# A selective-scan block on one core: decays of two states in one tile of two PSUM banks, and step sizes in the banks of the sums

## The chip, the core and the metric

The kernel runs on one core of a Trainium2 chip. The core has five engines that matter here, each with its own queue of instructions that it works off in order: PE multiplies matrices into PSUM, ACT applies functions to single elements, DVE does vector operations and scans, POOL does vector operations too, SP issues the DMAs. PSUM is used here as eight banks of 128 partitions x 512 float32 numbers. The metric is the device time in microseconds (us) of one execution: 11345.4 us is the median of three runs of the kernel before (11343.77 to 11359.79).

## What is computed

Eight images of 96 channels and 64 x 64 pixels go through a convolutional block with a selective scan, then through an attention block and a feed-forward block. The scan takes almost all the time. Each image is read as a sequence of L = 4096 pixels in four orders (k = 0 to 3: by windows row-wise, by windows column-wise, and both backwards). For each order, each of 192 channels d and each of 16 states n:

```python
dts, bs, cs = (x_dbl[:, :, :R], x_dbl[:, :, R:R + N], x_dbl[:, :, R + N:])
delta = jax.nn.softplus(dt_projs(dts) + dt_projs_b)
A = -jnp.exp(A_logs)
# one step in l
dA = jnp.exp(dt_i[..., None] * A)
hst = dA * hst + (dt_i * u_i)[..., None] * b_i[:, :, None, :]
y = jnp.einsum('bkdn,bkn->bkd', hst, c_i)
```

A decay dA and an input dt*u*b for every channel, state and pixel, a linear recurrence along the pixels, a product with c, and a sum over the states. What stands before the scan (norm, projections, a depthwise convolution) is called the front here, what follows it the back end.

## The kernel before, in words

**Units.** The work is cut into 256 units: 8 images x 2 pairs of orders x 2 directions x 8 chunks of T = 512 pixels. A unit holds 6 tiles (`TILES`, n = 0 to 5): for each half g of the states and each third j of the channels a tile `hb` of 128 partitions x 4 states x 512 pixels. The partitions are 64 channels x 2 states, so that four "states" m = 0 to 3 in the free dimension stand for eight of the reference's. A unit therefore has 24 slots, one per state of a tile, and 256 x 24 = 6144 scans are made in all.

**One slot** (lines 1112 to 1135). ACT computes the decay `exp(a * delta)` of the state two slots ahead into a bank of PSUM (`decays`, line 1055). DVE scans the present state (line 1123). Then the state has to be multiplied by c, and there are two ways:

- A *banked* state is scanned in place in its PSUM bank, and DVE multiplies it by c into `hb` (line 1125). ACT copies its last element into `carry` (line 1126), where the next unit's scan starts.
- A *plain* state is scanned into `hb`. When all four states of the tile are scanned, ACT copies the last elements (line 1131) and POOL multiplies the plain states of the tile by c in one instruction (`outputs`, line 948).

The table `BANKED` says how many states of each tile n are banked: 4, 0, 4, 0, 4 and 2, or 1 in the last tile in the first eight units of an image from the second image on. So it divides the products by c between DVE and POOL.

**The other steps of a unit.** `inputs` (line 942, POOL) multiplies b and dt*u for a whole tile, seven slots before its first scan. `sums` (line 962, PE) adds the states with a matrix of two identities in two accumulators, `y01` and `y2` (a bank each; tiles 0, 1, 3 and 4 in the first, 2 and 5 in the second); at the end it also adds the D*u term, or the y of the orders done before, from tiles that `before` (line 954) has loaded. `gather` (line 983, ACT) copies the two banks out, and a DMA stores them. `step_sizes` (line 901) makes softplus in six steps: a matmul into a bank `dt`, Abs, Exp and Ln on ACT, max-and-add on DVE (line 925), and the product with u on POOL (line 928). One call (a) makes 128 channels of a unit, another (b) the 64 remaining channels of two units. `spread` (line 930) copies the results into tiles that hold each channel twice, by DMA; `states` (line 873) loads b and c.

**Order.** The schedule is written out by hand: `plan` (line 997) puts each step of a unit u, of the unit before (`last`) and of the next two (`nxt`, `third`) into one of the 24 slots, and the engines' queues follow that order. Between the slots, `advance` (line 1086) issues the steps of two side streams: the back end of the image before and the front of the next image. Some of their activations need another function table; those are issued in the slots `CALM` = 0, 1, 8, 9, 16 and 17 alone (line 391). Requests for DMAs made by `later` go out three slots afterwards.

**Banks.** Of the eight banks, `da` has three (one state each, in rotation), `dt`, `f0`, `f1`, `y01` and `y2` one each; `f0` and `f1` serve the side streams.

Of the kernel before, what the change touches and what calls it, by code (L numbers as in the profile page):

```python
# [9 lines left out]
F32 = mybir.dt.float32  # L10
# [14 lines left out]
G = 4  # L25
# [8 lines left out]
BANKED = ((4, 0, 4, 0, 4, 1), (4, 0, 4, 0, 4, 2))  # L34
# [9 lines left out]
def kernel(ctx: ExitStack, tc: tile.TileContext, a, out):  # L44
# [16 lines left out]
    BANKS = {"da": 3, "dt": 1, "f0": 1, "f1": 1, "y01": 1, "y2": 1}  # L61
# [784 lines left out]
    for b in range(out.shape[0]):  # L846
        s = {"b": b, "done": set(), "live": b + 1 == out.shape[0]}
        images.append(s)
        for pair in (1, 0):
            for back in range(2):  # L850
                for i in range(NC):
# [4 lines left out]
                    u.bc, u.hb, u.delta, u.du = {}, {}, {}, {}  # L856
                    u.banked = BANKED[int(b == 0 or u.i % 32 >= NC)]
# [43 lines left out]
    def step_sizes(us, i):  # L901

        u, which = us[0], "ab"[len(us) - 1]
        if i == 0:
            u.ps = bank("dt", "dt")
# [42 lines left out]
    def outputs(u, n):  # L948

        lo = u.banked[n]  # L950
        hb = u.hb[n][:, lo:, :]
        nc.gpsimd.tensor_tensor(hb, hb, u.bc[1, TILES[n][0]][:, lo:, :], ALU.mult)  # L952

    def before(u):

        src = u.s["u"][1] if u.k == 1 else u.s["y"][u.pair]
        u.plain = []
        for i, rows in enumerate((slice(0, P), slice(P, src.shape[0]))):
            t = sp.tile([P, T], F32, tag=f"u{i}", name=f"u{i}", bufs=1)[: rows.stop - rows.start]
            u.plain.append(into(t, src[rows, bass.ts(u.c, T)]))  # L960

    def sums(u, ns, m):
# [12 lines left out]
        if ns[-1] == 5 and m == 1:  # L975
            first = u.k == 1
            for ps, w, x in (
                (u.p[0], dd_a if first else ident, u.plain[0]),
                (u.p[1][low] if first else u.p[1], dd_b if first else ident, u.plain[1]),
            ):  # L980
                nc.tensor.matmul(ps, w, x, start=False, stop=True, skip_group_check=True)  # L981
# [15 lines left out]
    def plan(u, last, nxt, third):  # L997
# [6 lines left out]
        if last:  # L1004
            put(0, outputs, last, 5)
            put(0, before, last)
            for m in range(2):
                put(m, sums, last, (3, 4), 2 + m)
            for m in range(2):
                put(5 + m, sums, last, (5,), m)  # L1010
            put(7, states, u, 1, 1)
            put(10, gather, last, 0)
            put(11, gather, last, 1)
# [4 lines left out]
        if third and u.i % 2:  # L1018
            put(16, step_sizes, (nxt, third), 5)
        put(8, outputs, u, 1)  # L1020
        put(16, outputs, u, 3)
        for m in range(4):
            put(13 + m, sums, u, (0, 1), m)
            if m < 2:
                put(18 + m, sums, u, (2,), m)
                put(22 + m, sums, u, (3, 4), m)
        if nxt:
            for i, slot in enumerate((0, 2, 4)):
                put(slot, step_sizes, (nxt,), i + 3)
            put(4, spread, nxt, 0, (0, 1))  # L1030
# [194 lines left out]
```

## Time and profile before

| | |
|---|---|
| median of three runs | 11345.4 us |
| the profiled execution | 11372.4 us, of which the profile's span is 11370.7 us |
| first to last scan | 351.6 to 11090.8 us |
| DVE busy, POOL busy, ACT busy | 10367.4 us, 10398.7 us, 7508.4 us |
| products by c on POOL (L952) | 512 of 4 states, 4529 ns each; 56 of 3, 3452 ns; 200 of 2, 2365 ns |
| products by c on DVE (L1125) | 3528 of one state, 692 ns each |
| scans (L1123) | 6144 |
| copies of ends on ACT | 3528 of one column (157 ns), 768 of a tile |
| mean granted clock of PE | 0.82 of full speed |

A line of the page's groups reads so: the source line, the engine, the operation, output tile <- input tiles, partitions x elements and type of both, the number of instructions; then their busy time in us and the mean length of one in ns; then the idle time of the engine just before them and what ended most of it. A line of the waits reads: who waited, <- for whom, then total us, number of waits, and the longest in us. A line of the timeline reads: start in us from the span's start, length in us, engine, line, operation, tiles; in brackets the idle time before it and what ended it. The page counts idle time on an engine only where nothing ran on it; two instructions of one engine can overlap, so the distance between starts can be shorter than a length.

### The profile page before, as it was taken

Reading aid. Unit: us, or ns where it says so; the run is one execution under the profiler, and the core shown is the slowest. Engines: PE = TensorE matmul, PEld = TensorE weight load, DVE = VectorE, ACT = ScalarE, POOL = GpSimd, SP = SyncE. Lnnn points to the kernel's source line nnn. Section 1 sums busy time; section 2 is a strip of 40 time slices with the busy share of each in tenths; the row PEclk is TensorE's granted clock in tenths of the full one; section 3 lists DMA queues with packets and bytes.
Section 4 is the critical chain, followed back from the end, with each engine's and each line's share of the span. In section 5 each row is a group of like instructions: output and inputs, shape, how many; then the busy total and the mean of one; then the engine's idle time right before and its main releaser. Section 6 shows DMA issues by size and latency. Waiting matters only on the chain. (4 is left out here: it accounts for less than half of the span.)

```text
span 11370.7 us, 97041 instructions
## 1 busy us (share of the span) xinstructions
PE 8567.3 (75%) x23270; PEld 2328.5 (20%) x23270; DVE 10367.4 (91%) x10828; ACT 7508.4 (66%) x14939; POOL 10398.7 (91%) x2783
## 2 busy tenths in 40 slices
PE   6577657887778877888678876788768887676677
PEld 2111112222122211222112221222212221111122
DVE  0799999999999999999999999999999999999991
ACT  3566656767666676667766676666766667666674
POOL 0799999999999999999999999999999999999990
PEclk8678778888788877889778887888878888787787
DMA  2788878898888888888888888889888888888872
GB/s 71 171 197 197 201 189 210 209 225 196 203 210 212 219 198 202 210 215 215 195 207 210 216 214 194 210 205 228 202 200 211 212 220 195 198 198 195 201 188 78
DMA packets 1081039, 2253.24 MB, mean 198 GB/s; under 512 B 419609, under 2 KB 420314, under 8 KB 949395
## 3 DMA queue, kind: packets, MB, share of 16 engines
q1 hardware_dynamic: 1080467, 2247.05, 81.3%
q8 instruction: 184, 3.01, 0.1%
q14 instruction: 388, 3.18, 0.1%
HBM read 1507.14 MB, written 336.69 MB: 162 GB/s over the span
## 5 line engine op out<-in xcount | busy, mean ns | idle before, releaser
L946 POOL TENSOR_TENSOR hb<-b,du 128x2048 f32<-128x2048 f32 x1536 | 6939.0, 4535 | 21.3 <-DMA du<-ua 14.3
L1062 ACT ACTIVATE da<-delta,w_a_logs 128x512 f32<-128x512 f32 x6144 | 4216.7, 689 | 696.3 <-DVE hb L1123 575.8
L972 PE MATMUL p<-hb,halves 128*64 128x512 f32 x12288 | 3822.7, 731 | 800.1 <-POOL hb L952 382.1
L1123 DVE TENSOR_TENSOR_SCAN da<-da,carry,hb 128x512 f32<-128x512 f32 x3087 | 3949.0, 1279 | 58.0 <-ACT da L1062 54.3
L952 POOL TENSOR_TENSOR hb<-hb,c 128x2048 f32<-128x2048 f32 (+2 forms) x768 | 2984.9, 3887 | 304.7 <-ACT carry L1131 252.2
L1123 DVE TENSOR_TENSOR_SCAN hb<-da,carry,hb 128x512 f32<-128x512 f32 x2289 | 2781.0, 1264 | 57.7 <-ACT da L1062 56.7
L1125 DVE TENSOR_TENSOR hb<-da,c 128x512 f32<-128x512 f32 x3528 | 2440.5, 692 | 154.0 <-DVE da L1123 0.9
L1126 ACT COPY carry<-da 128x1 f32<-128x1 f32 x3528 | 554.9, 157 | 2351.6 <-DVE hb L1125 2341.1
L972 PEld LDWEIGHTS p<-hb,halves 128*64 128x64 f32 x12288 | 916.2, 161 | 3540.7 <-issue 2129.5
L434 PE MATMUL conv<-f0im,taps 97*128 97x512 f32 (+1 forms) x2088 | 903.5, 664 | 95.9 <-ACT f0pre L490 54.3
L928 POOL TENSOR_TENSOR ua<-nat,ua 128x512 f32<-128x512 f32 x256 | 327.3, 1279 | 257.5 <-DMA b<-xd 257.5
L1123 DVE TENSOR_TENSOR_SCAN da<-da,hb 128x512 f32<-128x512 f32 x441 | 537.7, 1219 | 26.0 <-POOL hb L946 24.6
L925 DVE SCALAR_TENSOR_TENSOR nat<-dt,nat 128x512 f32<-128x512 f32 x384 | 259.5, 676 | 238.9 <-ACT nat L923 238.9
L911 PE MATMUL dt<-dts,dt_w 7*64 7x512 f32 (+1 forms) x1024 | 450.0, 657 | 16.9 <-DVE nat L925 12.4
L981 PE MATMUL p<-u,ident 128*128 128x512 f32 x768 | 438.3, 699 | 3.6 <-DMA u<-y 3.6
L376 PE MATMUL ctr<-f1b,cen_c 96*96 96x512 f32 x460 | 271.9, 697 | 193.4 <-DVE f1b L769 158.8
L434 PEld LDWEIGHTS conv<-f0im,taps 97*128 97x128 f32 (+1 forms) x2088 | 254.6, 174 | 681.6 <-issue 523.5
L1123 DVE TENSOR_TENSOR_SCAN hb<-da,hb 128x512 f32<-128x512 f32 x327 | 377.9, 1204 | 4.9 <-ACT da L1062 4.9
L382 PE MATMUL var<-f1b,ones_c 96*96 96x512 f32 x346 | 207.4, 684 | 153.6 <-ACT f1b L379 145.3
L792 POOL TENSOR_TENSOR f1b<-f1b,f1o 96x512 f32<-96x512 f32 x58 | 67.7, 1167 | 252.0 <-ACT f1o L790 251.9
L1131 ACT COPY carry<-hb 128x4 f32<-128x4 f32 (+2 forms) x768 | 146.8, 191 | 197.4 <-DVE hb L1123 184.8
L655 PE MATMUL cab<-f1m,cab_w 96*96 96x512 f32 x348 | 206.0, 719 | 90.9 <-ACT f1b L664 41.4
(416 smaller groups left out, 7710.5 us busy)
## 6 DMA issues: line engine op xcount, KB each, us to landing
b<-xd SPq DMA_DIRECT2D x1024, 512.0 KB
c<-xd SPq DMA_DIRECT2D x1024, 512.0 KB
delta<-nat SPq DMA_DIRECT2D x1536, 128.0 KB
du<-ua SPq DMA_DIRECT2D x1024, 128.0 KB
y<-yt SPq DMA_DIRECT2D x512, 256.0 KB
u<-y SPq DMA_DIRECT2D x384, 256.0 KB
ua<-u SPq DMA_DIRECT2D x256, 256.0 KB
du<-ub SPq DMA_DIRECT2D x512, 128.0 KB
```

The source lines that it names most:

```text
L376: nc.tensor.matmul(ps, cen_c, src, start=i == 0, stop=i == len(srcs) - 1)
L434: nc.tensor.matmul(ps, taps[:, t, lo : lo + n], im[:, r0 + dy : r0 + dy + 8, dx : dx + HW], start=t == 0, stop=t == 8,)
L911: nc.tensor.matmul(ps, dt_w[32 * w.k : 32 * w.k + R + 1, d], w.dts, start=True, stop=True)
L928: nc.gpsimd.tensor_tensor(x, u.nat, x, ALU.mult)
L946: nc.gpsimd.tensor_tensor(hb, u.bc[0, g], u.du[j].unsqueeze(1).to_broadcast([P, G, T]), ALU.mult)
L952: nc.gpsimd.tensor_tensor(hb, hb, u.bc[1, TILES[n][0]][:, lo:, :], ALU.mult)
L972: nc.tensor.matmul(ps, halves, u.hb[n][:, i, :], start=TILES[n][0] == 0 and m == 0, stop=False, skip_group_check=True)
L981: nc.tensor.matmul(ps, w, x, start=False, stop=True, skip_group_check=True)
L1062: nc.scalar.activation(da[q], u.delta[j], AF.Exp, scale=a_neg[:, u.k, j, g * G + m : g * G + m + 1])
L1123: nc.vector.tensor_tensor_scan(dd if banked else x, dd, x, 0.0 if u.start else col, ALU.mult, ALU.add)
L1125: nc.vector.tensor_tensor(hb[:, m, :], d, u.bc[1, g][:, m, :], ALU.mult)
L1126: kept.append(lambda col=col, d=d, at=first_at: nc.scalar.copy(col, d[:, at : at + 1]))
```

## The change

Four things change together. The decays of two states go into one tile of two neighbouring banks, of which two rotate (four banks instead of three); each scan still takes one state, but the product with c of two banked states is one instruction of 1024 elements, and one copy on ACT takes both ends. The bank `dt` goes: call (a) of the step sizes uses `y01`, call (b) `y2`, between the eviction of one unit's sums and the start of the next one's. For that, `plan` is laid out anew: the evictions come at slots 4 and 8, the step sizes between 6 and 20, the loads and DMAs move with them, and the sum of tiles 0 and 1 starts a slot later. And the table gives more states to DVE: the last tile has 2 banked states, and 4 in every second unit in the larger part of the images. In each `put` the first argument is the slot.

```diff
@@ -31,7 +31,7 @@
 SPREAD = 5
 HB = 6
 
-BANKED = ((4, 0, 4, 0, 4, 1), (4, 0, 4, 0, 4, 2))
+BANKED = (((4, 0, 4, 0, 4, 2),), ((4, 0, 4, 0, 4, 2), (4, 0, 4, 0, 4, 4)))
 
 HOLD = 3
 LAND = 11
@@ -58,7 +58,7 @@
     dram = ctx.enter_context(tc.tile_pool(name="scratch", bufs=2, space=DRAM))
     psum = ctx.enter_context(tc.tile_pool(name="psum", bufs=1, space=PSUM))
 
-    BANKS = {"da": 3, "dt": 1, "f0": 1, "f1": 1, "y01": 1, "y2": 1}
+    BANKS = {"f0": 1, "f1": 1, "y01": 1, "y2": 1}
 
     def bank(tag, name):
         return psum.tile([P, T], F32, tag=tag, name=name, bufs=BANKS[tag])
@@ -853,8 +853,9 @@
                     u.s, u.pair, u.back, u.k = s, pair, back, pair + 2 * back
                     u.c, u.start = (NC - 1 - i if back else i), i == 0
                     u.new, u.i = (pair, back, i) == (1, 0, 0), len(units)
-                    u.bc, u.hb, u.delta, u.du = {}, {}, {}, {}
-                    u.banked = BANKED[int(b == 0 or u.i % 32 >= NC)]
+                    u.bc, u.hb, u.delta, u.du, u.plain = {}, {}, {}, {}, {}
+                    some = BANKED[int(b == 0 or u.i % 32 >= NC)]
+                    u.banked = some[u.i % len(some)]
                     units.append(u)
 
     TILES = [(g, j) for g in range(2) for j in range(3)]
@@ -902,7 +903,7 @@
 
         u, which = us[0], "ab"[len(us) - 1]
         if i == 0:
-            u.ps = bank("dt", "dt")
+            u.ps = bank({"a": "y01", "b": "y2"}[which], "dt")
             if which == "a":
                 todo = [(u.ps, slice(0, P), u)]
             else:
@@ -948,16 +949,24 @@
     def outputs(u, n):
 
         lo = u.banked[n]
+        if lo == G:
+            return
         hb = u.hb[n][:, lo:, :]
         nc.gpsimd.tensor_tensor(hb, hb, u.bc[1, TILES[n][0]][:, lo:, :], ALU.mult)
 
-    def before(u):
+    def before(u, i):
 
         src = u.s["u"][1] if u.k == 1 else u.s["y"][u.pair]
-        u.plain = []
-        for i, rows in enumerate((slice(0, P), slice(P, src.shape[0]))):
-            t = sp.tile([P, T], F32, tag=f"u{i}", name=f"u{i}", bufs=1)[: rows.stop - rows.start]
-            u.plain.append(into(t, src[rows, bass.ts(u.c, T)]))
+        rows = (slice(0, P), slice(P, src.shape[0]))[i]
+        t = sp.tile([P, T], F32, tag=f"u{i}", name=f"u{i}", bufs=1)[: rows.stop - rows.start]
+        u.plain[i] = into(t, src[rows, bass.ts(u.c, T)])
+
+    def added(u, i):
+        ps, first = u.p[i], u.k == 1
+        w = ((dd_a, dd_b)[i]) if first else ident
+        nc.tensor.matmul(
+            ps[0:64] if first and i else ps, w, u.plain[i], start=False, stop=True, skip_group_check=True
+        )
 
     def sums(u, ns, m):
 
@@ -972,13 +981,6 @@
             nc.tensor.matmul(
                 ps, halves, u.hb[n][:, i, :], start=TILES[n][0] == 0 and m == 0, stop=False, skip_group_check=True
             )
-        if ns[-1] == 5 and m == 1:
-            first = u.k == 1
-            for ps, w, x in (
-                (u.p[0], dd_a if first else ident, u.plain[0]),
-                (u.p[1][low] if first else u.p[1], dd_b if first else ident, u.plain[1]),
-            ):
-                nc.tensor.matmul(ps, w, x, start=False, stop=True, skip_group_check=True)
 
     def gather(u, i):
 
@@ -1003,54 +1005,61 @@
 
         if last:
             put(0, outputs, last, 5)
-            put(0, before, last)
             for m in range(2):
                 put(m, sums, last, (3, 4), 2 + m)
+            put(2, added, last, 0)
+            put(4, gather, last, 0)
             for m in range(2):
                 put(5 + m, sums, last, (5,), m)
+            put(6, added, last, 1)
+            put(8, gather, last, 1)
             put(7, states, u, 1, 1)
-            put(10, gather, last, 0)
-            put(11, gather, last, 1)
+        if nxt:
+            put(2, spread, nxt, 0, (0, 1))
+            put(3, spread, nxt, 1, (0, 1))
+        if third:
+
+            put(5, fetched_u, third)
+            for i, slot in enumerate((6, 8, 9, 10, 12, 20)):
+                put(slot, step_sizes, (third,), i)
+            if u.i % 2:
+                for i, slot in enumerate((9, 11, 12, 13, 15, 16)):
+                    put(slot, step_sizes, (nxt, third), i)
         for n in range(6):
             to = (u, n + 2) if n < 4 else (nxt, n - 4)
             if to[0]:
                 put(4 * n + 1, inputs, *to)
-        if third and u.i % 2:
-            put(16, step_sizes, (nxt, third), 5)
         put(8, outputs, u, 1)
         put(16, outputs, u, 3)
-        for m in range(4):
-            put(13 + m, sums, u, (0, 1), m)
+        for m, slot in enumerate((14, 15, 16, 16)):
+            put(slot, sums, u, (0, 1), m)
             if m < 2:
                 put(18 + m, sums, u, (2,), m)
                 put(22 + m, sums, u, (3, 4), m)
+        put(18, before, u, 0)
+        put(21, before, u, 1)
         if nxt:
-            for i, slot in enumerate((0, 2, 4)):
-                put(slot, step_sizes, (nxt,), i + 3)
-            put(4, spread, nxt, 0, (0, 1))
-            put(6, spread, nxt, 1, (0, 1))
             put(10, states, nxt, 0, 0)
             put(15, states, nxt, 1, 0)
             put(20, states, nxt, 0, 1)
             if u.i % 2 == 0:
                 put(15, spread, nxt, 0, (2,))
                 put(16, spread, nxt, 1, (2,))
-        if third:
-            put(1, fetched_dt, third)
-            put(9, fetched_u, third)
-            for i, slot in enumerate((20, 22, 23)):
-                put(slot, step_sizes, (third,), i)
-            if u.i % 2:
-                for i, slot in enumerate((9, 11, 12, 13, 15)):
-                    put(slot, step_sizes, (nxt, third), i)
+            else:
                 put(17, spread, nxt, 0, (2,))
                 put(18, spread, nxt, 1, (2,))
-            elif u.i + 3 < len(units):
-                put(21, fetched_pair, third, units[u.i + 3])
+        fourth = at_index(u.i + 3)
+        if fourth:
+            put(14, fetched_dt, fourth)
+            if u.i % 2 == 0:
+                put(21, fetched_pair, third, fourth)
         return at
 
     def at_index(i):
         return units[i] if 0 <= i < len(units) else None
+
+    def column(j, g, m):
+        return 8 * j + g * G + m
 
     def decays(q):
 
@@ -1058,12 +1067,13 @@
             return
         u, (n, m) = units[q // 24], divmod(q % 24, G)
         g, j = TILES[n]
-        da[q] = bank("da", "da")
+        if m % 2 == 0:
+            da[q // 2] = psum.tile([P, 2, T], F32, tag="da", name="da", bufs=2)
         nc.scalar.activation(
-            da[q], u.delta[j], AF.Exp, scale=a_neg[:, u.k, j, g * G + m : g * G + m + 1]
+            da[q // 2][:, m % 2, :], u.delta[j], AF.Exp, scale=a_neg[:, u.k, j, g * G + m : g * G + m + 1]
         )
 
-    da, kept, side, carry = {}, [], [], None
+    da, kept, side, carry = {}, [], [], [None]
     for u in units[:2]:
         fetched_dt(u)
     fetched_u(units[0])
@@ -1076,12 +1086,43 @@
     for what in range(2):
         spread(units[0], what, range(3))
     fetched_u(units[1])
-    for i in range(3):
-        step_sizes(units[1:2], i)
     inputs(units[0], 0)
     inputs(units[0], 1)
     decays(0)
     decays(1)
+    for i in range(6):
+        step_sizes(units[1:2], i)
+    fetched_dt(units[2])
+
+    def scanned_state(u, slot):
+
+        n, m = divmod(slot, G)
+        g, j = TILES[n]
+        q, hb = 24 * u.i + slot, u.hb[n]
+        end = slice(0, 1) if u.back else slice(T - 1, T)
+        while kept:
+            kept.pop(0)()
+        decays(q + 2)
+        pair = da[q // 2]
+        d, x = pair[:, m % 2, :], hb[:, m, :]
+        banked = m < u.banked[n]
+        if u.back:
+            d, x = d[:, ::-1], x[:, ::-1]
+        col = column(j, g, m)
+        init = 0.0 if u.start else carry[0][:, col : col + 1]
+        nc.vector.tensor_tensor_scan(d if banked else x, d, x, init, ALU.mult, ALU.add)
+        if m % 2 == 0:
+            return
+        del da[q // 2]
+        if banked:
+            nc.vector.tensor_tensor(hb[:, m - 1 : m + 1, :], pair, u.bc[1, g][:, m - 1 : m + 1, :], ALU.mult)
+            ends, lo, hi = pair, m - 1, m + 1
+        elif m == G - 1:
+            ends, lo, hi = hb[:, u.banked[n] :, :], u.banked[n], G
+        else:
+            return
+        to = carry[0][:, column(j, g, lo) : column(j, g, hi)].unsqueeze(2)
+        kept.append(lambda: nc.scalar.copy(to, ends[:, :, end]))
 
     def advance(n):
 
@@ -1103,33 +1144,14 @@
                 final = back_end(b, u.s)
                 last_kit = back_kit(None, "f0", True, kit_f)
                 side.append(Stream(final[0][0](last_kit, range(1, NC)[::-1])))
-        if third and third.new:
+        if u.i + 3 < len(units) and units[u.i + 3].new:
             drained(*side[-1:])
             all_issued()
         if u.start:
-            carry = sp.tile([P, 24], F32, tag="carry", name="carry")
+            carry[0] = sp.tile([P, 24], F32, tag="carry", name="carry")
         todo = plan(u, last, nxt, third)
         for slot in range(24):
-            n, m = divmod(slot, G)
-            g, j = TILES[n]
-            q, hb, first_at = 24 * u.i + slot, u.hb[n], 0 if u.back else T - 1
-            col = carry[:, 8 * j + g * G + m : 8 * j + g * G + m + 1]
-            while kept:
-                kept.pop(0)()
-            decays(q + 2)
-            d = da.pop(q)
-            banked = m < u.banked[n]
-            dd, x = (d[:, ::-1], hb[:, m, ::-1]) if u.back else (d, hb[:, m, :])
-            nc.vector.tensor_tensor_scan(dd if banked else x, dd, x, 0.0 if u.start else col, ALU.mult, ALU.add)
-            if banked:
-                nc.vector.tensor_tensor(hb[:, m, :], d, u.bc[1, g][:, m, :], ALU.mult)
-                kept.append(lambda col=col, d=d, at=first_at: nc.scalar.copy(col, d[:, at : at + 1]))
-            elif m == G - 1:
-                lo = 8 * j + g * G
-                kept.append(
-                    lambda c=carry[:, lo + u.banked[n] : lo + G].unsqueeze(2), h=hb[:, u.banked[n] :, :], at=first_at:
-                    nc.scalar.copy(c, h[:, :, at : at + 1])
-                )
+            scanned_state(u, slot)
             for f, args in todo[slot]:
                 f(*args)
             place[0] = slot
...
```

More of the change, by code (lines that the diff above doesn't have):

```diff
@@ L1140 @@
     outputs(u, 5)
-    before(u)
     for m in range(2):
@@ L1145 @@
         sums(u, (5,), m)
+    for i in range(2):
+        added(u, i)
     gather(u, 0)
```

## The prediction

> **What bounds the kernel now.** I read the page from the top: the engines' shares, the slices, the groups by line; then the waits of DVE and of POOL, and a stretch of the timeline. The chain that ended last has 2% of the span and carries nothing here.
>
> ```profile
> PE 8567.3 (75%) x23270; PEld 2328.5 (20%) x23270; DVE 10367.4 (91%) x10828; ACT 7508.4 (66%) x14939; POOL 10398.7 (91%) x2783
> ```
> Two engines are full; the slices show 9 for both except at the ends. Their groups, and ACT's largest:
>
> ```profile
> L946 POOL TENSOR_TENSOR hb<-b,du 128x2048 f32<-128x2048 f32 x1536 | 6939.0, 4535 | 21.3 <-DMA du<-ua 14.3
> L1062 ACT ACTIVATE da<-delta,w_a_logs 128x512 f32<-128x512 f32 x6144 | 4216.7, 689 | 696.3 <-DVE hb L1123 575.8
> ...
> L1123 DVE TENSOR_TENSOR_SCAN da<-da,carry,hb 128x512 f32<-128x512 f32 x3087 | 3949.0, 1279 | 58.0 <-ACT da L1062 54.3
> ...
> L1125 DVE TENSOR_TENSOR hb<-da,c 128x512 f32<-128x512 f32 x3528 | 2440.5, 692 | 154.0 <-DVE da L1123 0.9
> ```
> Which of the two leads is in DVE's waits:
>
> ```profile
> DVE hb L1123 <- ACT da L1062: 61.6, 90, 1.4
> ...
> DVE da L1123 <- ACT da L1062: 54.3, 22, 6.0
> ...
> DVE da L1123 <- POOL hb L946: 25.1, 8, 20.2
> ```
> DVE hardly waits for POOL; POOL waits 252.2 us for L1131, the copy of ends that follows DVE's scans. So **DVE leads** and POOL is close behind. From the first scan to the last (351.6 to 11090.8 us) DVE's gaps sum to 338 us: 117 end with a decay, 25 with POOL, most of the others with an input from ACT or PE for the neighbouring images' work.
>
> What a state costs DVE is read from starts, since its instructions overlap:
>
> ```profile
> 5016.39 1.28 DVE L1123 TENSOR_TENSOR_SCAN da<-da,carry,hb 128x512 f32<-128x512 f32 x1
> 5016.51 0.16 ACT L1126 COPY carry<-da 128x1 f32<-128x1 f32 x1 [1.63 <-DVE hb L1125]
> 5016.70 0.69 ACT L1062 ACTIVATE da<-delta,w_a_logs 128x512 f32<-128x512 f32 x1
> ...
> 5017.71 0.69 DVE L1125 TENSOR_TENSOR hb<-da,c 128x512 f32<-128x512 f32 x1
> ...
> 5018.31 1.28 DVE L1123 TENSOR_TENSOR_SCAN da<-da,carry,hb 128x512 f32<-128x512 f32 x1
> ```
> The product needs the scan's result and starts 1.32 us after it (median over the trace 1.316). The next scan needs nothing of the product and starts 0.60 later (median 0.608), before the product has ended. Scans into hb, which don't depend on each other, follow at 1.176. A banked state thus takes 1.924 us of DVE, a plain one 1.176. ACT's copy and decay come after the product has ended: that releases the bank.
>
> **DVE's work.** The new table makes 156 units of 14 banked states and 100 of 16: 3784 instead of 3528. At the old price 256 more cost 256 x 0.748 = +191 us. Pairing changes the price. In the order of the changed kernel's instructions the second scan of a banked pair waits for the first one's end, because both write one tile. The trace has no scan waiting for a scan; its ends are 1.176 (free) and 1.316 (as the product waits). A wait for a result of the same length is the nearer row: 1.316. The product of 1024 elements has rows on both sides, 692 ns at 512 and 1957 ns at 1728 (L227), so 1.22 us long; from start to next start 0.608 + 0.533 (512 elements at the 1.04 ns of these rows) = 1.141, or 1.22 if nothing overlaps. I take 1.141. A pair: 1.316 + 1.316 + 1.141 = 3.773, against 2 x 1.924 = 3.848: 0.075 less, times 1892 pairs = -142. In 165 pairs another instruction stands between the scans and hides the 0.14 of the wait: -23. **Sum +26 us.** Ends: 1727 x 0.14 = 242 less with a free wait, 1892 x 0.08 = 150 more without overlap.
>
> [...] But the row of starts shows that the fixed part is half covered already (0.608 between starts, not 0.692), so 0.075 is left, and I use the row.
>
> **POOL's work.** 200 products of two states and 56 of three become 156 of two; from the rows by shape (4529, 3452, 2365 ns) 2985 - 2688 = 297 us less. DVE gains only its 25 us of gaps behind POOL: **-25**.
>
> **The decays' lead.** This is where I expect the loss. Before, three banks rotate and a scan waits for its own decay; ACT may be two states ahead. After, two pairs rotate. A pair's first decay waits until the pair before last is multiplied and its ends are copied, and the first scan of a pair waits for both decays (the order's waits show it). Between the two decays stands everything ACT has to do in the even slot. From the start of a pair's first scan, ACT can begin after 0.11, copies (0.19), makes two decays (0.69 + 0.72, the second waits for the first): 1.71 us. A banked pair lasts 3.77 and leaves 2.06 for other work, a plain one 2.35 and leaves 0.64 (0.83 without copy). The largest other work is a table load, an activation, a table load: 1.29 + 1.50 + 1.29 = 4.08 us, in quiet slots. Before, it had 3 x 1.924 less 1.84 (start and copies 0.49, two decays 1.35) = 3.93 us and cost 0.15; now, in an even slot, it costs 2.0. Taking the ACT rows that stand between the two decays in the order, with their intervals from the trace, they exceed what is left in 61 of 1891 banked windows, by 116 us together (53 of them such bursts), and in 148 of 1180 plain ones, by 65. That is 181 us. Of the 117 of today 35 end at slot 11, where ACT itself waits for PE, and stay; 82 are replaced. **+99.** Ends: +30, if the bursts meet idle stretches; +190, since work after the second decay, left out here, can push the next pair too. ACT gains 1636 copies less (0.19 each, 311 us); these are taken into the windows.
>
> **Banks of the sums.** The step sizes' product moves from slot 20 to slot 6 of the same unit, into y01, and b's takes y2. So the sums must be evicted at slots 4 and 8 instead of 10 and 11. Behind the copy at slot 8 stand on ACT the Abs of the step sizes, which waits for its PE product, and the next decays. Today ACT waits 6.6 us in all for L981: there was room. Read in the timeline for the fourth image, the last tile-5 sum ends after the next unit's slot 8 begins in 9 units of 32, on average 1.5 us after. Then come one added product and the dt product (1.1 each), against 1.1 us that the pair has left beside copy and Abs: up to 1.7 us each, 9 x 8 x 1.7 = 122; nothing, if PE, with one added product less ahead, is on time. PE loses work there, so I take under half: **+55**. Sums (0,1) start a slot later and end close to where POOL refills their buffer (slot 17); POOL's 297 us hide it, and without them two or three units in 32 would cost about 1 us each.
>
> **Moved at no cost.** The other steps of a (Abs to max-add) come at 8 to 12 instead of 22 to 2; ACT's are counted in the windows, DVE's is the same instruction. POOL's ua product moves from slot 4 to slot 20 before, seven slots (12 us) ahead of the DMA that takes it. Delta and du go out at slots 2 and 3, not 4 and 6: SP's 1951.7 us of waiting for L925 go, which nothing that DVE waits for was behind. The u and y loads (18, 21) have 8 slots, some 14 us, until their product; dts (14) has 16, ua (5) 15. Were such a load late, SP's queue behind it would be, and the sums. The front stages end in unit 26 of an image, before the drain, which now comes at 29 instead of 30.
>
> Sum: 26 + 99 + 55 - 25 = +155 us. The profiled execution took 11372.4, with 11370.7 of span, 27 above the median 11345.4; I add the step to the median: **11500**.
>
> **Rivals.**
> *POOL sets the pace through others.* DVE's gaps other than for decays are 221 us; if POOL's fullness stands behind them (POOL was busy 284.32 of 284.32 us in the window from 6822 us; PE waits 382.1 for L952), they go: 11345 + 26 - 221 = 11150. Against it: the gaps end with ACT and PE results of side work. It decides if decays cost under 195.
> *The second scan's wait is nearly free.* 11500 - 242 = 11258. [...] Against: the product[...] waits 1.316.
> *It cancels.* The copies saved give ACT room for its bursts: 11345 + 26 - 25 = 11346. Against: the buffers, not ACT's load, bound the lead.
> *The tight order costs more.* Upper ends, 26 + 190 + 122 - 25: 11660, and to 11800 with the product unoverlapped.
>
> **Chances.** Main case 11400 to 11600: 0.60; tight order 0.22; cancels 0.07; POOL 0.05; free wait 0.06. What this kernel's measurement can tell is about 0.2%: same is 11323 to 11368. Faster 0.11, same 0.06, slower 0.83. The range for 8 in 10, 11340 to 11680, leaves out the two faster cases and the tail of the tight one.
>
> **What would show it.** In the new profile: starts of two banked scans 1.32 apart and 1.14 from product to next scan; DVE's busy time about as now; POOL's near 10100; DVE waiting 200 us or more for decays, at even slots only, above all 2, 10 and 18; ACT waiting for the added product. Wrong if DVE's wait for decays stays near 116, or DVE's scans of a pair start 1.18 apart.

## The result, and the profile after

The changed kernel takes **11480.7 us** (median of four runs, 11471.39 to 11484.81), the kernel before 11350.56 beside it (four runs, 11343.77 to 11359.79). The ratio is 1.0115, with a 95% interval of 1.0102 to 1.0127: 130 us slower, where 155 were forecast.

The profiled execution has a span of 11469.7 us, 99 more than the one before. From the first scan to the last it takes 10861.6 us (351.8 to 11213.3) instead of 10739.2: **+122**. Behind the last scan it takes 256.4 instead of 279.9. That part is 256 to 266 in the later runs too, and 256 in one that keeps the old layout (`e6_order_alone`), so most of the 27 us by which the profiled execution of before lay above its median seems to stand there. The 122 us between the scans are what has to be explained.

The page's first part, and its costliest groups:

```profile
PE 8559.5 (75%) x23270; PEld 2303.9 (20%) x23270; DVE 10415.6 (91%) x9192; ACT 7268.9 (63%) x13203; POOL 10109.5 (88%) x2683
...
L947 POOL TENSOR_TENSOR hb<-b,du 128x2048 f32<-128x2048 f32 x1536 | 6926.7, 4527 | 46.9 <-PE p L981 22.8
L1113 DVE TENSOR_TENSOR_SCAN da<-da,carry,hb 128x512 f32<-128x512 f32 x3336 | 4285.1, 1285 | 247.1 <-ACT da L1072 150.5
L1072 ACT ACTIVATE da<-delta,w_a_logs 128x512 f32<-128x512 f32 x6144 | 4227.9, 689 | 396.8 <-DVE hb L1113 263.1
...
L1118 DVE TENSOR_TENSOR hb<-da,c 128x1024 f32<-128x1024 f32 x1892 | 2317.1, 1225 | 95.9 <-DVE da L1113 0.9
```

DVE executes 1636 instructions fewer and is busy 48 us longer. POOL has lost 289 us, and ACT 240. The idle time before the banked scans has grown from 58.0 us to 247.1, and the decays end most of it. In the waits of DVE, where both kinds of scan and the largest wait for side work between the scans stand:

```profile
DVE da L1113 <- ACT da L1072: 150.5, 99, 4.7
...
DVE f1b L571 <- ACT f1b L570: 52.7, 80, 2.6
DVE hb L1113 <- ACT da L1072: 46.6, 55, 2.9
```

From the start of the first scan to that of the last, decays end 201 us of DVE's gaps instead of 117, and POOL 12 instead of 5. All gaps in this stretch sum to 390 us instead of 318, **+72**; the rest of the 122 us, **+51**, is DVE's own work (gaps under 0.04 us, such as the one before a product, count as work). A wait for POOL before the first scan, 20.2 us in the kernel before and 2.4 now, stands outside this stretch. POOL now waits behind DVE (before, 252.2 us):

```profile
POOL hb L955 <- ACT carry L1125: 595.8, 278, 7.8
```

How a pair goes, in the timeline of DVE (rows alike that follow each other are joined, so x2 with 2.62 us is two scans):

```profile
4997.10 2.62 DVE L1113 TENSOR_TENSOR_SCAN da<-da,carry,hb 128x512 f32<-128x512 f32 x2 [1.12 <-ACT da L1072]
4999.75 1.22 DVE L1118 TENSOR_TENSOR hb<-da,c 128x1024 f32<-128x1024 f32 x1
5000.89 2.61 DVE L1113 TENSOR_TENSOR_SCAN da<-da,carry,hb 128x512 f32<-128x512 f32 x2
5003.53 1.22 DVE L1118 TENSOR_TENSOR hb<-da,c 128x1024 f32<-128x1024 f32 x1
```

The product starts 2.65 us after the first scan, and the next scan 1.14 after the product's start. Two scans of a pair start 1.316 us apart (median of 1727), two scans into `hb` 1.190: the second of a pair does wait for the first. And the 1.12 us of idle time in the first row is what the prediction feared. ACT's timeline just before shows its cause:

```profile
4991.80 0.69 ACT L1072 ACTIVATE da<-delta,w_a_logs 128x512 f32<-128x512 f32 x1
4992.50 1.28 ACT L397 ACT_TABLE_LOAD   x1
4993.80 0.68 ACT L631 ACTIVATE gm<-cab,cab_b 64x512 f32<-64x512 f32 x1
4994.50 1.28 ACT L397 ACT_TABLE_LOAD   x1
4995.79 0.69 ACT L490 ACTIVATE f0pre<-conv,cb_a 128x512 f32<-128x512 f32 x1
4996.38 0.68 ACT L1072 ACTIVATE da<-delta,w_a_logs 128x512 f32<-128x512 f32 x1
```

The first and the last row are the decays of one pair. Between them stand two table loads and two activations of the side streams, 3.9 us. The scan at 4997.10 needs only the first of the two decays for its arithmetic, yet it starts when the second is ready (4996.38 + 0.68 = 4997.06), since both lie in one tile.

### The profile page after: what moved, and what is told of

Its sections match the earlier page's. It is cut to its first block, busy times and chain, and to the rows that moved or that the text cites. A ratio compares the mean times of both kernels' runs of the same rounds, so it can differ in the third digit from the quotient of the medians.

```text
span 11469.7 us, 93727 instructions
## 1 busy us (share of the span) xinstructions
PE 8559.5 (75%) x23270; PEld 2303.9 (20%) x23270; DVE 10415.6 (91%) x9192; ACT 7268.9 (63%) x13203; POOL 10109.5 (88%) x2683
## 5 line engine op out<-in xcount | busy, mean ns | idle before, releaser
L1113 DVE TENSOR_TENSOR_SCAN da<-da,carry,hb 128x512 f32<-128x512 f32 x3336 | 4285.1, 1285 | 247.1 <-ACT da L1072 150.5
L981 PE MATMUL p<-hb,halves 128*64 128x512 f32 x12288 | 3627.0, 710 | 684.3 <-DVE nat L926 467.3
L955 POOL TENSOR_TENSOR hb<-hb,c 128x2048 f32<-128x2048 f32 (+1 forms) x668 | 2685.9, 4021 | 601.5 <-ACT carry L1125 595.8
L1113 DVE TENSOR_TENSOR_SCAN hb<-da,carry,hb 128x512 f32<-128x512 f32 x2040 | 2496.9, 1265 | 49.8 <-ACT da L1072 44.8
L1118 DVE TENSOR_TENSOR hb<-da,c 128x1024 f32<-128x1024 f32 x1892 | 2317.1, 1225 | 95.9 <-DVE da L1113 0.9
L1125 ACT COPY carry<-da 128x2 f32<-128x2 f32 x1892 | 300.6, 159 | 2704.4 <-DVE hb L1118 2703.0
L912 PE MATMUL dt<-dts,dt_w 7*128 7x512 f32 (+1 forms) x1024 | 520.2, 769 | 385.3 <-ACT yt L994 210.8
L1125 ACT COPY carry<-hb 128x4 f32<-128x4 f32 (+1 forms) x668 | 129.5, 194 | 455.7 <-DVE hb L1113 438.6
L618 PE MATMUL cab<-f1im,cab_w 97*32 97x512 f32 x1044 | 283.0, 665 | 24.7 <-DVE f1pad L597 17.3
L929 POOL TENSOR_TENSOR ub<-nat,ub 128x512 f32<-128x512 f32 x128 | 162.7, 1271 | 140.1 <-DVE nat L926 137.3
```

The costliest lines, as they stand in the source:

```text
L618: nc.tensor.matmul(ps[at : at + 32, :], cab1_w[:, t, :], k.im.t[:, 8 * q + dy : 8 * q + dy + 8, dx : dx + HW], start=t == 0, stop=t == 8, ...
L912: nc.tensor.matmul(ps, dt_w[32 * w.k : 32 * w.k + R + 1, d], w.dts, start=True, stop=True)
L929: nc.gpsimd.tensor_tensor(x, u.nat, x, ALU.mult)
L981: nc.tensor.matmul(ps, halves, u.hb[n][:, i, :], start=TILES[n][0] == 0 and m == 0, stop=False, skip_group_check=True)
L1113: nc.vector.tensor_tensor_scan(d if banked else x, d, x, init, ALU.mult, ALU.add)
L1118: nc.vector.tensor_tensor(hb[:, m - 1 : m + 1, :], pair, u.bc[1, g][:, m - 1 : m + 1, :], ALU.mult)
```

## The experiments

My theory before these runs was the prediction's: the joined tile costs through the decays' lead, since one tile for two states makes a scan wait for both decays and binds the second scan to the first, and the table costs because DVE, not POOL, is the bound. The rival: the new layout with its early evictions costs, and the pairing is worth having. All times are medians of four runs (ten for `e4_table_14`), each with the median of the kernel before on the same chip.

### Single banks instead of pairs

Same layout and table; the four banks are four tiles, and every state has its own product and copy again.

```diff
-    BANKS = {"f0": 1, "f1": 1, "y01": 1, "y2": 1}
+    BANKS = {"da": 4, "f0": 1, "f1": 1, "y01": 1, "y2": 1}
...
-        if m % 2 == 0:
-            da[q // 2] = psum.tile([P, 2, T], F32, tag="da", name="da", bufs=2)
+        da[q] = bank("da", "da")
...
-            nc.vector.tensor_tensor(hb[:, m - 1 : m + 1, :], pair, u.bc[1, g][:, m - 1 : m + 1, :], ALU.mult)
+            nc.vector.tensor_tensor(hb[:, m, :], d, u.bc[1, g][:, m, :], ALU.mult)
```

> The changed layout and table, but each decay has a bank of its own (four in rotation) and each banked state its own product straight after its scan, as before. Pairing's part alone is undone. Theory (DVE's work and ACT's lead set the time): a banked state costs 1.924 us of DVE again, 165 us more than the pairs in all; the waits for decays fall from 201 us to about 50, since a scan waits for its own decay alone and four banks rotate. Together about +15: 11495 us (11440 to 11560). Rival (the loss lies in the new layout of evictions and step sizes): the waits stay near 200 us and DVE's extra work comes on top: 11645.

Measured: 11422.1 us, before 11352.0, ratio 1.0063 (1.0048 to 1.0078). That is below the expected range: DVE works 119 us more than in the changed kernel, not 165, and the gaps fell by more than was expected of the decays alone. Decays end 54 us of the gaps:

```profile
DVE da L1111 <- ACT da L1071: 30.6, 18, 3.3
...
DVE hb L1111 <- ACT da L1071: 22.8, 22, 3.3
```

All gaps are 213 us instead of 390. So **joined tile and joined product together lose 176 us of waiting for 119 us of work saved**. That the sum over both is still above before must come from the table or the layout.

### The table, and the layout

Here the second entry of the table is taken back, so that all units have 14 banked states:

```diff
-BANKED = (((4, 0, 4, 0, 4, 2),), ((4, 0, 4, 0, 4, 2), (4, 0, 4, 0, 4, 4)))
+BANKED = (((4, 0, 4, 0, 4, 2),), ((4, 0, 4, 0, 4, 2),))
```

> The changed kernel with 14 banked states in every unit. Theory (DVE is the bound): 100 units have two banked states less, each pair 3.773 - 2.352 = 1.42 us, so DVE has 142 us less and the time falls by about as much, 11340 us (11310 to 11400), although POOL gets 100 products of 2365 ns more (10346 us busy). Rival (POOL is the bound): no gain, or up to 200 us slower.

Measured: 11328.9 us, before 11352.0, ratio 0.9979 (0.9970 to 0.9988), 152 us less than the changed kernel. 100 pairs of states went back to POOL, and DVE's work between the scans fell by 142 us, the 1.42 us a pair that was expected. POOL's busy time rose by 227 us and cost nothing; it ends 9 us of DVE's gaps, where it ended 12: **DVE is the bound, POOL had room**.

```profile
PE 8576.4 (76%) x23270; PEld 2301.0 (20%) x23270; DVE 10279.1 (91%) x9092; ACT 7260.2 (64%) x13203; POOL 10336.8 (91%) x2783
```

The next has single banks as the first experiment, and the table of before: the layout, with one bank more for decays, is all that is left of the change.

```diff
-BANKED = (((4, 0, 4, 0, 4, 2),), ((4, 0, 4, 0, 4, 2), (4, 0, 4, 0, 4, 4)))
+BANKED = (((4, 0, 4, 0, 4, 1),), ((4, 0, 4, 0, 4, 2),))
```

> e1_single_banks with the table of before (14 banked states, 13 in 56 units): of the change only the new layout is left, which frees a bank, so that four single decays rotate. Theory: 256 states fewer on DVE at 0.748 us are 191 us less than e1, and the waits for decays stay near 54 us, against 117 before: about 11240 us (11200 to 11290), a gain over the kernel before of some 110; then the loss of the change is table and pairing together. Rival (the early evictions cost as much as the fourth bank gains): 11330 or more.

Measured: 11220.2 us, before 11343.6, ratio 0.9888 (0.9874 to 0.9903). Decays' waits are 52 us, all gaps 200 instead of 318. The layout is not what costs; with a fourth single bank it gains. The layout with three banks was not run, so the two parts of this gain are not told apart; the waits for decays are 65 of the 118 us of gaps that went.

So the change comes apart into three, each taken against the kernel before on its own chip:

| step | us |
|---|---|
| layout, and a fourth bank for single decays (`e5_layout_alone`) | -123 |
| 256 more states multiplied by DVE (to `e1_single_banks`: +70) | +193 |
| decays and products of two states joined (to the changed kernel: +130) | +60 |

### What the joined product itself is worth

The tiles stay joined; only the product is split again. This is the direct test of the price that the prediction took from the row of starts, 0.075 us a pair. If joining saved the whole fixed part of a product, it would be 0.159: an estimate from two lengths of the trace before, 692 ns at 512 elements and 1957 at 1728, which is 1.04 ns an element and 0.159 us beside them.

```diff
-            nc.vector.tensor_tensor(hb[:, m - 1 : m + 1, :], pair, u.bc[1, g][:, m - 1 : m + 1, :], ALU.mult)
+            for i in range(2):
+                nc.vector.tensor_tensor(hb[:, m - 1 + i, :], pair[:, i, :], u.bc[1, g][:, m - 1 + i, :], ALU.mult)
```

> The changed kernel, its pair of decays in one tile as it is, but the product of a pair in two instructions of 512. Nothing else moves. Theory (of the fixed part of a product only what isn't overlapped is saved): 0.590 + 0.608 us between starts in e2 against 1.141, 0.06 to 0.075 us per pair, 1892 pairs: 110 to 140 us slower than the changed kernel, 11605 us (11570 to 11640). [...]

Measured: 11586.5 us, before 11354.5, ratio 1.0204 (1.0189 to 1.0219): 106 us more than the changed kernel, 0.056 us for each of 1892 products. In the profiles DVE's work between the scans grows by 117 us, 0.062 each, and the gaps are 346 us instead of 390. In DVE's timeline of this kernel:

```profile
5004.65 2.61 DVE L1113 TENSOR_TENSOR_SCAN da<-da,carry,hb 128x512 f32<-128x512 f32 x2
5007.30 1.29 DVE L1119 TENSOR_TENSOR hb<-da,c 128x512 f32<-128x512 f32 x2
```

Two products take 1.29 us from start to end, not twice 0.69; the pair starts 2.65 us after its scans as before, and the next scan starts 1.20 after the first product, where the joined one leaves 1.14. So joining does not save the whole fixed part of 0.159 us: the second of two products starts 0.60 us after the first, 0.09 before that one has ended.

This run also splits the last row of the table. Against `e1_single_banks` it has the same products of one state, and DVE's work is the same (10589 and 10591 us), but the tiles and the copies of the ends are joined: 164 us slower, and in the profiles the gaps are 346 us instead of 213. So the joined tile costs about 160 us and the joined product gains about 100, each taken against the kernel before on its own chip.

### The other way to use four banks: scan, scan, product, product

If the wait of an instruction for the one just before it costs 0.14 us (1.316 against 1.176), it is better to separate them than to join them. With single banks, the two scans don't depend on each other, and neither do the products; each product then stands one instruction behind its scan. The four single tiles are made as in the first experiment.

```diff
...
         if m % 2 == 0:
             return
-        del da[q // 2]
+        ds = [da.pop(q - 1), da.pop(q)]
         if banked:
-            nc.vector.tensor_tensor(hb[:, m - 1 : m + 1, :], pair, u.bc[1, g][:, m - 1 : m + 1, :], ALU.mult)
+            for i, d in enumerate(ds):
+                nc.vector.tensor_tensor(hb[:, m - 1 + i, :], d, u.bc[1, g][:, m - 1 + i, :], ALU.mult)
...
```

> As e1_single_banks, but the order on DVE is scan, scan, product, product, each state with its own tile. No instruction then follows directly the one it waits for. Theory (0.14 us is lost wherever a dependent instruction follows its source at once, and the joined product saves only 0.075): two states take 2 x 1.176 + 2 x 0.608 = 3.568 us, 388 us less than the pairs, 530 less than e1. DVE's work falls under POOL's 10110 us, so that POOL joins in as bound: about 11050 us (10950 to 11150), with scans of a pair starting 1.18 apart. Rival (one product of 1024 elements is what pays): slower than the changed kernel, 11600.

Measured: **10932.6 us**, before 11352.0, ratio 0.9632 (0.9616 to 0.9648), better than expected. Its first line on the page and its DVE timeline:

```profile
PE 8368.8 (77%) x23270; PEld 2267.0 (21%) x23270; DVE 10121.0 (93%) x11084; ACT 7215.2 (66%) x15095; POOL 10103.4 (93%) x2683
```

```profile
5001.58 2.46 DVE L1111 TENSOR_TENSOR_SCAN da<-da,carry,hb 128x512 f32<-128x512 f32 x2
5003.94 1.27 DVE L1117 TENSOR_TENSOR hb<-da,c 128x512 f32<-128x512 f32 x2
5005.13 2.46 DVE L1111 TENSOR_TENSOR_SCAN da<-da,carry,hb 128x512 f32<-128x512 f32 x2
```

From pair to pair it takes 3.55 us instead of 3.78: scan to scan 1.190, scan to product 1.175, product to product 0.590, product to scan 0.594 (medians). DVE has 1892 instructions more than in the changed kernel and is busy 295 us less. Against the single states of the first experiment (1.317 + 0.608 each) a state costs 0.15 us less; times 3784 that is 568, and 490 came out: DVE's work between the scans fell by 522 us, and the gaps grew from 213 to 238.

The run of the last section, `e9_product_split`, gives DVE the same scans and products in the same order. Only the tiles of two states and the joined copies of their ends are different there, and it takes 654 us more: in the profiles 520 of work and 109 of gaps. With joined tiles the second scan starts 1.316 us after the first and the product 1.325 after the second scan, and the order gains nothing; with single tiles the same two intervals are 1.190 and 1.175. So in this order **the joined tile is what costs**, for it makes each of these instructions wait for the one just before it.

The same order alone, in the kernel before: three single banks, the old layout, table and bank `dt`. The decay of the state after next must here wait for the products, so its call moves behind them in the odd slots of banked states.

```diff
-            decays(q + 2)
...
+            if not (last_of_two and m < u.banked[n]):
+                decays(q + 2)
...
+            if banked and (last_of_two or m + 1 == u.banked[n]):
+                for m1 in range(m - last_of_two, m + 1):
+                    d1 = da.pop(q + m1 - m)
+                    nc.vector.tensor_tensor(hb[:, m1, :], d1, u.bc[1, g][:, m1, :], ALU.mult)
...
+                if last_of_two:
+                    decays(q + 2)
...
```

> The kernel before, with its layout, table and three banks, but two banked states in turn: scan, scan, product, product. The decay of the state two after the second scan is issued after the first product, whose bank it takes. Theory (a dependent instruction right behind its source costs 0.14 us): 3528 x 0.14 = 494 us less on DVE, of which 100 go back in waits for decays with three banks; POOL, with its 10400 us, becomes the bound: 11000 to 11150, 11080. Rival (three banks don't bear it): the waits for decays rise by more than 400 us and nothing is gained.

Measured: 11206.2 us, before 11343.6, ratio 0.9878 (0.9863 to 0.9893): above the expected range, and a third of the gain. DVE's work does fall (busy 10028.7 us), and its waits take the place:

```profile
DVE da L1126 <- POOL hb L946: 141.1, 133, 22.0
DVE hb L1126 <- ACT da L1062: 114.3, 163, 1.9
DVE da L1126 <- ACT da L1062: 100.1, 82, 7.1
```

Of 442 us of work that went between the scans, 296 came back as gaps. The decays' waits grew by the 100 us that I had expected of three banks. The 141 behind POOL (22 of them before the first scan) I had not expected: with POOL at 10391.3 us of busy time, DVE has caught up with it. The other gaps grew by 80. That the larger table, useless in the changed kernel, has its place here, and the fourth bank too, is inferred from these waits: `e2_two_scans_two_products` has layout, fourth bank and table together, and they were not added one by one.

### Taking the decays' wait away by order

The next three ask whether the 201 us come off by moving ACT's work, with the pairs kept. First, both decays of a pair are issued one after the other at the even slot.

```diff
-        decays(q + 2)
+        if m % 2 == 0:
+            decays(q + 2)
+            decays(q + 3)
```

> The changed kernel, with both decays of the next pair issued at the even slot, before the rest of that slot's work on ACT. Theory (what ACT does between the two decays holds up the first scan of the next pair): a table load, activation, table load of 4.08 us now falls after the second decay and has 2.06 + 2.06 us; the waits for decays fall from 201 us to 60 to 90, those at slots 2, 10 and 18 from 151 to under 60: 11360 us (11310 to 11420). Rival (ACT waits for PE at the early evictions, or ACT has too much to do): the waits move to other slots and the time stays at 11480.

Measured: 11464.8 us, before 11352.0, ratio 1.0102 (1.0087 to 1.0117). Not as expected. The waits for decays went to 69 us as meant, but the sum of all gaps stayed 389, against 390:

```profile
DVE f1b L571 <- ACT f1b L570: 114.6, 86, 2.9
...
DVE hb L1115 <- ACT da L1072: 51.8, 31, 4.8
...
DVE f1b L586 <- PE attn L584: 43.0, 19, 5.7
```

Where decays go first, what ACT makes for the side streams comes late, and DVE meets that in its own queue. The wait for decays was an account of *which* of ACT's results came late.

Second, the table switches are allowed in the odd slots 1, 9 and 17 only, after both decays of a pair.

```diff
-    CALM = (0, 1, 8, 9, 16, 17)
+    CALM = (1, 9, 17)
```

> The changed kernel, with table loads and the activation between them allowed in slots 1, 9 and 17 alone, so that no burst falls between the two decays of a pair. Theory: the 115 us of waits with such a burst before them fall to under 40, those at slots 2, 10 and 18 from 151 to under 70, and, unlike in e3, nothing else is put off on ACT: 11390 us (11350 to 11430). Rival (as in e3, DVE's side work waits instead): 11465 to 11480.

Measured: 11539.4 us, before 11343.6, ratio 1.0174 (1.0157 to 1.0191): slower than the changed kernel. The decays that wait for a burst (a table load with the activation between) fell from 115 us to 36 as meant; all decays' waits are still 164. And one short instruction of the back end had become long. In the timeline:

```profile
5124.23 15.18 DVE L693 TENSOR_SCALAR dgate<-ident,gate 96x96 f32<-96x96 f32 x1
5124.72 4.51 POOL L955 TENSOR_TENSOR hb<-hb,c 128x2048 f32<-128x2048 f32 x1
5129.19 4.48 POOL L947 TENSOR_TENSOR hb<-b,du 128x2048 f32<-128x2048 f32 x1
5133.64 1.25 POOL L929 TENSOR_TENSOR ua<-nat,ua 128x512 f32<-128x512 f32 x1
5134.86 4.48 POOL L947 TENSOR_TENSOR hb<-b,du 128x2048 f32<-128x2048 f32 x1
5139.34 2.48 DVE L1113 TENSOR_TENSOR_SCAN da<-da,hb 128x512 f32<-128x512 f32 x2
```

An instruction of 96 numbers per partition begins 0.5 us before POOL ends one instruction, and it ends when POOL has worked off four more in a row. It did so in six of the eight images, 92.4 us in all against 14.3 in the changed kernel, and the scans behind it waited with it. To tell this from the order of ACT, the same kernel was run with this one instruction on ACT:

```diff
-            nc.vector.tensor_scalar(dgate, ident[:C, :C], gate, None, ALU.mult)
+            nc.scalar.activation(dgate, ident[:C, :C], AF.Identity, scale=gate)
```

> e7_bursts_odd, and the 96x96 scaling of the identity by the gate (L693), which took 15.2 us of DVE in six images of e7 while POOL worked without a pause, is made by ACT. Theory (DVE was held there by POOL, and the bursts' waits fell as meant): 92 us of DVE's time go, 11450 us (11430 to 11475), 20 to 40 under the changed kernel. Rival (the 15 us only showed a wait that something else imposes): above 11510.

Measured: 11456.0 us, before 11354.5, ratio 1.0092 (1.0076 to 1.0109): 83 us less than with it on DVE (94 if each is taken against the kernel before on its chip), about its 92. Against the changed kernel 25 are gained, 14 of which are the instruction itself. The decays' waits are still 163 us, with 89 of them at slot 10, and all gaps are 390 as in the changed kernel. Moving ACT's bursts doesn't mend the pairs either.

### The same moves with single banks

The order scan, scan, product, product (the diff of `e2_two_scans_two_products`) with the switches in odd slots (that of `e7_bursts_odd`):

> e2_two_scans_two_products with the bursts in slots 1, 9 and 17 alone. Theory: of its 95 us of waits for decays 62 have a burst before them; they go: 10880 us (10840 to 10920). Rival (POOL is the bound by now, 10103 us busy in 10307 between first and last scan): no change, 10930.

Measured: 10994.2 us, before 11343.6, ratio 0.9695 (0.9678 to 0.9712): above the expected range, and 62 us more than `e2_two_scans_two_products`. L693 took about 15.5 us in five images and 85 us in all, against 18 there, which accounts for the loss; the waits for decays are 100 us against 95, so that the switches in odd slots gain nothing here either. The last run is `e2_two_scans_two_products` with that instruction on ACT, and with the switches where they were, in all six slots:

```diff
-            nc.vector.tensor_scalar(dgate, ident[:C, :C], gate, None, ALU.mult)
+            nc.scalar.activation(dgate, ident[:C, :C], AF.Identity, scale=gate)
```

> e2_two_scans_two_products with L693 on ACT as in e10. There it took 2.55 us in seven images: 18 us less at most, 10915 us (10900 to 10935).

Measured: **10905.0 us**, before 11354.5, ratio 0.9607 (0.9592 to 0.9621). It is the fastest of all: DVE 10102.1 and POOL 10102.0 us busy, 97 us of waits for decays. Of the 28 us that it gains on `e2_two_scans_two_products`, 18 are L693; where the others come from stays open. It beats the kernel before by 3.9% and the changed one by 5%.

## Why the prediction was right

It said 11500, and 11480.7 came. Its terms one by one:

**What bounds the kernel: right.** DVE led and still leads. Taking 200 states off DVE gave back 152 us and loading POOL with them cost nothing (`e4_table_14`). POOL's busy time of 10109.5 is the "near 10100" of the text.

**DVE's work: right in kind, too small.** Forecast +26, measured +51. The second scan waits, at the 1.316 that was taken from the nearer row; from the product to the next scan 1.141 was taken and 1.141 to 1.142 measured. The term that was mis-sized is the product's wait for the pair: 1.325 us instead of 1.316, 17 us over 1892 pairs. About 8 more are not assigned to an instruction. The choice of the row held: splitting the product cost 0.056 to 0.062 us for each, nearer to 0.075 than to the estimate of 0.159 for a whole fixed part, with which the sum would have been 191 - 301 - 23 = -133 and have missed by 184.

**POOL: right in its own work, wrong in what that is worth to DVE.** POOL lost 289 us, 297 were forecast. The -25 for DVE could not come: 20.2 of the 25.1 us are one wait, the longest in the row that the prediction shows, and it ends at the first scan; the stretch from the first scan to the last does not contain it, and the first scan starts at 351.8 us where it started at 351.6. Without it the 338 us of gaps are 318, and in the stretch 5 us of gaps behind POOL became 12.

**The decays' lead: right in place and mechanism, too large by 31 of 99.** "DVE waiting 200 us or more for decays, at even slots only, above all 2, 10, and 18": it was 201 us, at even slots only, 23, 75 and 53 of them at 2, 10 and 18. The pairs that wait for a table switch cost 115 us in 61 windows, where 116 in 61, 53 of them with such a switch, had been counted out of the old trace. Those of plain states with other ACT work between cost 35 in 87, where 65 in 148 had been counted: this is the term that was mis-sized. Less the 82 that were replaced, that is +68, against +99.

**Early evictions: the weakest step.** +55 was forecast. ACT does wait for PE at both new places:

```profile
ACT yt L994 <- PE p L967: 59.9, 51, 5.5
ACT nat L920 <- PE dt L912: 59.4, 72, 4.1
```

These were 6.6 and 2.8 us before. But of the decays' waits only 51 us stand behind such a wait of ACT, against 36 before: **+15**. ACT's own waits there, 119 us, are near the 122 of the estimate, which was then cut to under half; but most of them don't reach DVE at all. That the lead of two decays takes them up is likely and not shown.

Together the waits are +84 for decays and +7 behind POOL; the other gaps fell by 19, and the sum is +72 where +129 was forecast. The forecast step thus was 57 us too large in the waits and 25 too small in the work. Within the waits the -25 for POOL hid a part of the excess for decays and evictions. The mechanism was right, but that the sum came as near as 155 to 130 is in part luck: these errors cancel.

**What the prediction did not see** is that the change holds a gain of 123 us: the same banks, freed by the same layout and used singly. It compared the change with the kernel before, not with the best use of the bank that it frees. And `e3_both_decays_first` and `e10_bursts_odd_gate_on_act` show that the wait for decays, once counted, is not a debt that can be paid by putting decays first: in both, the order of ACT only chose what DVE waits for, and the gaps stayed at 389 and 390 us. With tiles of one bank the lead comes back by itself, for a scan waits for its own decay alone: 54 us of waits, with the order of ACT's decays as it was (`e1_single_banks`).

## What to carry to other kernels

Ask of a joined buffer what it binds: one tile of two banks made a scan wait for a decay that it didn't need, and for the scan before it, and with the same order of instructions on DVE it took 654 us more than two tiles of one bank. Before joining instructions to save their fixed cost, read from the starts how much of it the following instruction covers already; putting an independent instruction between two dependent ones gave here 0.13 us a state (490 over 3784), joining their products 0.06 us a pair. And compare sums of gaps, not single waits: when one wait goes away while the sum stays, as here, reordering the engine behind it has only moved the wait.

## What the runs showed of the hardware

L693, a multiplication by a scalar, is 0.27 us long in the last image, where POOL is idle, and about 2.5 elsewhere before the change, where it ends 0.06 to 0.07 us after the POOL instruction that was running when it began. In `e7_bursts_odd` it is 15 us long in six images, where it begins 0.5 to 0.8 us before POOL ends an instruction that others follow without a pause. The tile's rows (count: shortest/median/longest in ns), before and in that run:

```profile
L693 DVE TENSOR_SCALAR dgate<-ident,gate x8: 268/2482/2491, 2348.0 to 11230.9; 96x96 f32<-96x96 f32 x8
```

```profile
L693 DVE TENSOR_SCALAR dgate<-ident,gate x8: 266/15168/15441, 2364.1 to 11401.0; 96x96 f32<-96x96 f32 x8
```

But in one image of the same run, with the same instructions of POOL around it, it ended with the one that ran when it began, 0.1 us after the next had started:

```profile
9260.44 0.58 DVE L693 TENSOR_SCALAR dgate<-ident,gate 96x96 f32<-96x96 f32 x1
9260.92 4.52 POOL L955 TENSOR_TENSOR hb<-hb,c 128x2048 f32<-128x2048 f32 x1
```

So L693 is long only where POOL works beside it. But in six images it did not end with the POOL instruction that ran when it began: four more, 4.51, 4.48, 1.25 and 4.48 us in the timeline above, went by. In one image it did. So it is not always held off when POOL's instructions follow without a pause; what decides that, and by what means POOL would hold it, these runs don't show. That the cost goes when the instruction leaves DVE, they do show: 83 us less, or 94 against the kernels before, where it had taken 92 (`e10_bursts_odd_gate_on_act`).
